# Mamba stage: accumulating transfers for two sums, eight pooled products, and writes on other queues

## The chip, the cores and the metric

The kernel runs on one core of a Trainium2 chip. That core has a matrix engine (TensorE, PE in the profile), three engines for elementwise work (VectorE or DVE, ScalarE or ACT, GpSimd or POOL), and SyncE (SP), which here only issues transfers. Sixteen DMA engines carry the transfers of all queues. Every engine works through its own instructions in order and waits on semaphores for the others. The metric is the device time of one execution in microseconds (us); for the kernel before, the median of three runs is 4138.68, between 4136.19 and 4147.42.

## The reference

The input is one image, 64 x 64 points with 256 channels, in float32. Layer 0 is a group norm, convolutions to q, k and v, attention and a projection. Layer 1 begins with a bidirectional Mamba block over the 4096 points as tokens, and ends with a mixture of experts. The change lies in the Mamba block, of which each direction computes, for 512 inner channels d and 16 states s:

```python
dt = jax.nn.softplus(jnp.einsum('blr,dr->bld', dt, dt_proj_w) + dt_proj_b)
A = -jnp.exp(A_log)
dA = jnp.exp(dt[..., None] * A)
dBx = dt[..., None] * Bm[:, :, None, :] * xc[..., None]
def step(h, inp):
    dA_t, dBx_t, C_t = inp
    h = dA_t * h + dBx_t
    y = jnp.einsum('bds,bs->bd', h, C_t)
    return (h, y)
```

Here xc is the input after a short convolution and silu, and Bm, Cm and the first factor of dt come from one projection of xc. The softplus is computed as relu(v) plus a correction plus log(1 + exp(-|v|)); the sum with that logarithm is one of the sums of the title. After both directions, m = forward + backward goes through a norm and a small two-layer network p, and the token becomes x1 + m + p, with x1 the block's input; the sum with x1 is the other one.

## The kernel before

The kernel has four stages, one after the other: convolutions, attention, Mamba (`mamba_phase`), experts. The change touches `mamba_phase` and the helper `layer_norm` (L101).

The 4096 tokens are cut into 8 chunks of 512. A **turn** i (0 to 15) is one chunk in one direction. A turn has 32 **slots**, one for each group of states and channels: e (4 groups of 128 channels), k (4 groups of states) and j (0 or 2), so that one slot covers two tiles of 128 x 512. The number of a slot in its turn is called `at`. For slot n the functions do the following:

- `inflow(n)` (L1853, its product L1859) is GpSimd's product dbx = (dt times x) times B. It is issued two slots ahead and has three buffers.
- `decay(n)` (L1841, L1849) is ScalarE's exponential da, issued one slot ahead.
- `recur(n)` (L1865) is VectorE's scan (L1872) over 1024 elements, and its product of the states with C (L1877). In the slots of the set `POOLED` the scan writes straight into the tile h, and GpSimd does the product with C one slot later (`pooled`, L1879).
- `sum_states` (L1905) sums the states on TensorE into y, and `close` (L1919) multiplies y by z on VectorE at the end of each e.
- `carry` (L1448) brings the old state into the next turn. It has a product on GpSimd (part 0), an exponential on ScalarE (part 1) and a second product on GpSimd (part 2). It needs the first value of dt of each row, which GpSimd copies to `first` (L1430), and which travels to DRAM-side rows and back to all partitions (L1433, `load_first` L1442).

`prepare(q)` (L1324) is a generator that computes what turn q needs, one step in each slot of the turn before and in the last five of the turn before that. Near its end it takes the logarithm (L1401, slot 23), and then spreads `dt_piece` over slots 24 to 29: with v = 0 GpSimd adds the logarithm to dt (L1425), with v = 1 it multiplies dt by xc (L1436) and adds a large number to the first column of odd rows (L1438), and SP writes both products to the scratch `dtd` in DRAM (L1440). Two of the four pieces with v = 1 are left to slots 2 and 4 of turn q itself. `load_dt` (L1473) reads `dtd` back, each row to four partitions, into the tiles dtr (for `decay`) and dtxr (for `inflow`), three buffers each. For the next group e it is issued at k = 1 and k = 2, slots 3 and 5 of each eight. The writes of B and C to the scratch `bcd` (L1367) and the loads from it (L1469) are on SP's queue also.

`tail(c)` (L1504) is the small network of a chunk, spread over two turns in slots where the set `FULL` allows the engine that its next step names. It has two `layer_norm`s, and each sends a row of 512 values through DRAM-side rows (L127, L129) to have the power taken on 128 partitions (L132). x1 is loaded by SP (L1510) and added to m by GpSimd (L1517).

The order of instructions on all engines is the order in which the program issues them (`manual_schedule`); nothing is moved by a planner. Turn 0 is prepared by `start` (L1551) instead of `prepare`, with parts of its work on VectorE.

Of the kernel before, what the change touches and what calls it, by code (L numbers as in the profile page):

```python
# [14 lines left out]
FP = mybir.dt.float32  # L15
# [4 lines left out]
ALU = mybir.AluOpType  # L20
AX = mybir.AxisListType
# [3 lines left out]
P = 128  # L25
# [3 lines left out]
CT = C // P  # L29
N = 512  # L30
NCH = NT // N
# [6 lines left out]
ET = DI // P  # L38
DS = 16
# [22 lines left out]
def step(gen, n=1):  # L62

    for _ in range(n):
        if gen is None or next(gen, StopIteration) is StopIteration:
            return False
    return True
# [30 lines left out]
        return self.small[:, a : a + n]  # L98


def layer_norm(cx, pool, new_psum, src, dst, mul=None, rest=0, centred=False):  # L101

    nc = cx.nc
    xc = src
    if not centred:  # L110
        ps = new_psum()
        for t in range(CT):
            nc.tensor.matmul(ps, cx.mean_mat, src[:, t, :], start=t == 0, stop=t == CT - 1)
        yield "DVE"
        xc = pool.tile([P, CT, N], FP, name="ln_xc", tag="ln_xc", bufs=1)
        nc.vector.tensor_tensor(xc, src, ps[:, None, :].to_broadcast([P, CT, N]), ALU.subtract)
    yield "ACT"
    nc.scalar.activation(dst, xc, AF.Square)
    yield "PE"
    ps = new_psum()  # L120
    for t in range(CT):
        nc.tensor.matmul(ps, cx.mean_mat, dst[:, t, :], start=t == 0, stop=t == CT - 1)
    yield "ACT"
    rstd = pool.tile([P, N], FP, name="ln_rstd", tag="ln_rstd", bufs=1)
    nc.scalar.activation(rstd[0:1, :], ps[0:1, :], AF.Identity, bias=cx.eps[0:1, :])
    row = cx.rows.tile([1, N], FP, name="ln_row", tag="ln_row", bufs=2)
    nc.sync.dma_start(out=row, in_=rstd[0:1, :])  # L127
    few = pool.tile([P, N // P], FP, name="ln_few", tag="ln_few", bufs=1)
    nc.sync.dma_start(out=few, in_=row.rearrange("o (p j) -> (o p) j", p=P))  # L129
    for at in range(1 + rest):  # L130
# [1092 lines left out]
def mamba_phase(cx, early, w_in, w_x, w_out, w1, w2, x1d, ud, bcd, dtd, x2d, u2d, usum):  # L1223
# [11 lines left out]
    nc, tc = cx.nc, cx.tc  # L1235
    with ExitStack() as ctx:
        one = ctx.enter_context(tc.tile_pool(name="c_one", bufs=1))
# [14 lines left out]
        halos = one.tile([P, 2, ET, 3], FP, name="halos")  # L1252
        nc.gpsimd.memset(halos, 0.0)

        odd = one.tile([P, 2], FP, name="odd")
        nc.vector.tensor_reduce(odd, cx.ident.rearrange("p (a b) -> p b a", b=2), AX.X, ALU.add)
        nc.vector.tensor_scalar(odd[:, 1:2], odd[:, 1:2], 1e33, None, ALU.mult)
        nc.vector.memset(odd[:, 0:1], 0.0)
        for d in range(2):
            for lst, have, src, shape, nm in (  # L1260
                (win, early.win, w_in, [P, CT, 2 * DI], "win"), (wx, early.wx, w_x, [P, ET, DR + 2 * DS], "wx"),
# [5 lines left out]
                t_ = one.tile(shape, FP, name=f"{nm}{d}")  # L1267
# [53 lines left out]
        def few():  # L1321
            return sp.tile([P, N], FP, name="few", tag="few", bufs=3)

        def prepare(q):  # L1324
# [38 lines left out]
            xd = few()[0:nx, :]  # L1363
            nc.scalar.copy(xd, ps[0:nx, :])

            at = 0 if d else DR
            nc.sync.dma_start(out=bcd[q], in_=xd[at : at + 2 * DS, :])  # L1367
            yield


# [31 lines left out]
            zs = in_pair(q, ET)  # L1402
            yield
            got["dt"] = dt
            for at, (v, e) in enumerate(((0, 0), (1, 0), (0, 1), (0, 2), (0, 3), (1, 1))):
                if at == 3 and q > 1:
                    load_first(q, 0)
                dt_piece(q, v, e, ex)
                if at in (0, 2):
                    z = sp.tile([P, 2, N], FP, name="z", tag="z", bufs=3)  # L1410
                    got.setdefault("z", []).append(z)
                if at < 4:
                    nc.scalar.copy(z[:, at % 2, :], zs[at % 2])  # L1413
                if at == 1:
                    zs = in_pair(q, ET + 2)
                    if q + 1 < 2 * NCH:
                        load_u(q + 1)
                yield

        def dt_piece(q, v, e, ex=None, eng=nc.gpsimd):  # L1420


            dt, xc = gots[q]["dt"], gots[q]["xc"]
            if v == 0:
                eng.tensor_tensor(dt[:, e, :], dt[:, e, :], ex[:, e, :], ALU.add)  # L1425
                if q < 2:
                    return
                if e == 0:
                    firsts[q] = ip.tile([P, ET], FP, name="first", tag="first", bufs=1)
                nc.gpsimd.tensor_tensor(firsts[q][:, e : e + 1], dt[:, e, 0:1], odd[:, 0:1], ALU.add)  # L1430
                if e % 2:
                    first_rows[q, e // 2] = cx.rows.tile([P, 2], FP, name="first_row", tag="first_row", bufs=2)
                    nc.sync.dma_start(out=first_rows[q, e // 2], in_=firsts[q][:, e - 1 : e + 1])  # L1433
            else:
                x = few()
                eng.tensor_tensor(x, dt[:, e, :], xc[:, e, :], ALU.mult)  # L1436

                eng.tensor_tensor(dt[:, e, 0:1], dt[:, e, 0:1], odd[:, 1:2], ALU.add)  # L1438
                for w, piece in enumerate((dt[:, e, :], x)):
                    nc.sync.dma_start(out=dtd[2 * q + w][e].rearrange("p j n -> (p j) n"), in_=piece)  # L1440

        def load_first(q, h):  # L1442

# [28 lines left out]

        def load_dt(i, e, j):  # L1473

            tiles = []
            for v, nm in enumerate(("dtr", "dtxr")):
                t_ = dtp.tile([P, 2, N], FP, name=nm, tag=nm)
                rows = dtd[2 * i + v][e, :, j : j + 2, :].rearrange("p j n -> p (j n)")
                nc.sync.dma_start(
                    out=t_.rearrange("p j n -> p (j n)"), in_=rows[:, None].to_broadcast([32, 4, 2 * N])  # L1480
                )
                tiles.append(t_)
            dts[i, e, j] = tiles

        def output(i):
# [18 lines left out]
        def tail(c):  # L1504

            m = m_of[c]
            hn = tl.tile([P, CT, N], FP, name="hn", tag="hn")
            yield from layer_norm(cx, tl, tl_psum, m, hn, nc.gpsimd, 2)
            x1 = tl.tile([P, CT, N], FP, name="x1", tag="ln_xc")
            nc.sync.dma_start(out=x1, in_=x1d[c])  # L1510
            for t in range(CT):
                nc.scalar.activation(
                    hn[:, t, :], hn[:, t, :], AF.Identity, scale=cx.col("lng", t), bias=cx.col("lnb", t)
                )
            yield "DMA"
            yield "POOL"
            nc.gpsimd.tensor_tensor(m, x1, m, ALU.add)  # L1517
            yield "PE"
            a1 = [
                tl.tile([P, 2, N], FP, name="a1a", tag="ln_xc"), tl.tile([P, 2, N], FP, name="a1b", tag="a1b"),  # L1520
# [1 line left out]
            for f in range(FT):  # L1522
# [5 lines left out]
                a = a1[f // 2][:, f % 2, :]  # L1528
# [3 lines left out]
            x2 = m  # L1532
# [10 lines left out]
                )  # L1543
            nc.sync.dma_start(out=x2d[c], in_=x2)
            u2 = tl.tile([P, CT, N], FP, name="u2", tag="hn")
            yield from layer_norm(cx, tl, tl_psum, x2, u2, nc.gpsimd, 2)
            nc.sync.dma_start(out=u2d[c], in_=u2)
            nc.vector.tensor_reduce(usum[:, :, c : c + 1], u2, AX.X, ALU.add)
            yield "DMA"
# [285 lines left out]
            (i, e, k, j) for i in range(2 * NCH) for e in range(ET) for k in range(SQ) for j in (0, 2)  # L1835
        ]
        SPS = ET * SQ * 2
        firsts, first_rows, got_first, brought = {}, {}, {}, {}
        gots, bcs, dts, m_of, das, us, ys, hs = {}, {}, {}, {}, {}, {}, {}, {}

        def decay(n):  # L1841
# [79 lines left out]
            nc.vector.tensor_tensor(g[:, e, :], ys.pop((i, e)), z[e // 2][:, e % 2, :], ALU.mult)  # L1921

        there = set()
        CARRY = {30: (0, 0), 31: (0, 2), 9: (1, 0), 11: (1, 2)}


        POOLED = {4, 10, 12, 18, 28}

        AHEAD = 5

# [11 lines left out]
        with tc.manual_schedule(engines=ORDERED):  # L1942
# [4 lines left out]
            tails, prep, out, last = [], None, None, None  # L1947
            for n, (i, e, k, j) in enumerate(slots):
                at = n % SPS
# [42 lines left out]
                if at >= SPS - AHEAD and i + 2 < 2 * NCH:  # L1992
                    coming = coming or prepare(i + 2)
                    step(coming)
                if i > 0 and at in (2, 4):
                    dt_piece(i, 1, 2 if at == 2 else 3)
                if at == 1 and i > 1:
                    load_first(i, 1)
                elif at in (10, 30) and 1 < i + (at > 16) < 2 * NCH:
                    carry(i + (at > 16), at < 16, 1)  # L2000
                if i == 2 * NCH - 1 and at in (4, 5, 6, 7, 10, 11, 12, 13, 15, 19, 21, 23, 25, 27, 28, 29, 30):
                    last = last or ahead()
# [314 lines left out]
```

## Time and profile before

| what | us |
|---|---|
| median of 3 runs | 4138.68 |
| the profiled execution's own time | 4145.32 |
| its span, first to last instruction | 4143.5 |
| TensorE busy in the span | 3629.8 |
| VectorE busy | 3490.9 |
| ScalarE busy | 2665.3 |
| GpSimd busy | 1748.2 |
| Mamba scans, first to last start | 1964.8 to 3832.1 |

A row of the profile names a source line, an engine, an operation and the tiles written and read. It then gives the shape and the count, and after the bar the busy time in us, the mean of one in ns, and the idle time of the engine just before these instructions with what ended it. Rows of a timeline begin with the start and the duration in us. The time from the issue of a transfer to its landing is known in this trace for those that GpSimd issues.

### The profile page before, as it was taken

The page shows a single profiled execution, that of the slowest core. Times are in us where ns is not written, and L with a number is a line of the kernel's source. Part 1 is how long each engine was busy: PE and PEld are TensorE (multiplying, and loading weights), DVE is VectorE, ACT ScalarE, POOL GpSimd, SP SyncE. Part 2 cuts the span into 40 slices and gives each one's busy share as a digit, 9 for nine tenths or more (in the row PEclk, how much of TensorE's full clock was granted, in tenths as well). Part 3 has the DMA queues.
Part 4 walks back from the last instruction along what each step waited for, and adds up shares of the span by engine and source line. Part 5 has one row for each costly group of instructions (what it writes and reads, how often), then busy time and mean ns, then how long its engine had stood idle before and what let it go on. Part 6 is the DMA issues. An engine that isn't in the chain of part 4 may idle for free. (4 is left out here: it accounts for less than half of the span.)

```text
span 4143.5 us, 43697 instructions
## 1 busy us (share of the span) xinstructions
PE 3629.8 (88%) x15176; PEld 1192.0 (29%) x15176; DVE 3490.9 (84%) x2886; ACT 2665.3 (64%) x4146; POOL 1748.2 (42%) x1189
## 2 busy tenths in 40 slices
PE   6769888999999999998888888888888888876898
PEld 2223332222222222222222222222222232221343
DVE  8998787889879879778899999999999999999211
ACT  1111226878878878776777778778787778775122
POOL 3020000000000000000888889888898989887000
PEclk9889998999999999999889899888989899888899
DMA  6232213000000000002334344343334444432221
GB/s 206 93 111 94 69 65 129 11 27 19 17 24 19 17 24 19 11 22 86 110 114 131 116 123 133 117 126 119 121 109 125 131 120 121 132 110 84 75 67 38
DMA packets 150517, 350.68 MB, mean 85 GB/s; under 512 B 35477, under 2 KB 44437, under 8 KB 150030
## 3 DMA queue, kind: packets, MB, share of 16 engines
q1 hardware_dynamic: 139198, 312.65, 24.6%
q0 software_dynamic: 11088, 35.14, 2.5%
q8 instruction: 121, 1.98, 0.2%
q14 instruction: 110, 0.90, 0.1%
HBM read 268.16 MB, written 79.56 MB: 84 GB/s over the span
## 5 line engine op out<-in xcount | busy, mean ns | idle before, releaser
L1859 POOL TENSOR_TENSOR dbx<-dtxr,b 128x1024 f32<-128x1024 f32 x512 | 1202.7, 2360 | 200.9 <-DMA dtxr<-dtd 106.3
L1016 ACT ACTIVATE e<-sc 128x1024 f32<-128x1024 f32 x1024 | 992.5, 1023 | 200.3 <-PE sc L1009 158.2
L1872 DVE TENSOR_TENSOR_SCAN da<-da,state,dbx 128x1024 f32<-128x1024 f32 x432 | 1014.4, 2348 | 19.4 <-ACT da L1849 7.0
L935 DVE TENSOR_TENSOR s<-s,e 128x1024 f32<-128x1024 f32 x768 | 881.1, 1224 | 45.1 <-ACT e L1016 44.7
L1849 ACT ACTIVATE da<-dtr,aneg 128x512 f32<-128x512 f32 x1024 | 708.2, 692 | 38.4 <-DMA dtr<-dtd 9.1
L1009 PE MATMUL sc<-q,kS 32*128 32x512 f32 x4096 | 652.1, 642 | 11.7 <-ACT e L1016 7.2
L132 POOL TENSOR_TENSOR ln_few<-ln_few,minus_half 128x4 f32<-128x4 f32 x29 | 29.5, 1017 | 1407.7 <-DMA ln_few<-ln_row 1407.7
L1877 DVE TENSOR_TENSOR h<-da,c 128x1024 f32<-128x1024 f32 x432 | 529.2, 1225 | 33.1 <-PE y L1912 1.2
L942 PE MATMUL av<-e,vT 128*32 128x512 f32 x4096 | 548.1, 606 | 3.7 <-ACT o L948 3.7
L1912 PE MATMUL y<-h,sel 128*32 128x512 f32 x2048 | 373.9, 665 | 97.4 <-DVE h L1877 71.6
L453 PE MATMUL cv<-v,u 128*128 128x512 f32 x928 | 412.4, 605 | 27.9 <-DVE pad L274 13.8
L1009 PEld LDWEIGHTS sc<-q,kS 32*128 32x128 f32 x4096 | 211.2, 183 | 455.3 <-issue 233.5
L1306 PE MATMUL mm<-u,win 128*128 128x512 f32 x464 | 253.7, 697 | 77.2 <-ACT z L1413 33.1
L453 PEld LDWEIGHTS cv<-v,u 128*128 128x128 f32 x928 | 178.8, 194 | 259.2 <-issue 226.8
L551 DVE SCALAR_TENSOR_TENSOR acc<-pad,wdw_s,acc 128x768 f32<-128x768 f32 (+1 forms) x192 | 236.0, 1234 | 19.9 <-ACT acc L544 14.2
L1903 ACT COPY state<-da 128x2 f32<-128x2 f32 x431 | 67.9, 158 | 257.4 <-DVE h L1877 256.2
L1352 PE MATMUL mm<-xp,taps 128*128 128x512 f32 x480 | 212.8, 595 | 0.0
L935 DVE TENSOR_TENSOR s<-e 128x1024 f32<-128x1024 f32 x128 | 151.2, 1225 | 65.3 <-ACT e L1016 65.1
L1872 DVE TENSOR_TENSOR_SCAN h<-da,state,dbx 128x1024 f32<-128x1024 f32 x80 | 187.5, 2344 | 11.0 <-ACT state L1903 9.8
L942 PEld LDWEIGHTS av<-e,vT 128*32 128x32 f32 x4096 | 81.2, 108 | 395.4 <-issue 377.7
L1882 POOL TENSOR_TENSOR h<-h,c 128x1024 f32<-128x1024 f32 x80 | 188.3, 2354 | 1.0 <-ACT state L1903 1.0
L1912 PEld LDWEIGHTS y<-h,sel 128*32 128x32 f32 x2048 | 56.6, 113 | 380.5 <-DVE h L1877 163.7
(381 smaller groups left out, 3933.4 us busy)
## 6 DMA issues: line engine op xcount, KB each, us to landing
dtr<-dtd SPq DMA_DIRECT2D x128, 512.0 KB
dtxr<-dtd SPq DMA_DIRECT2D x128, 512.0 KB
b<-bcd SPq DMA_DIRECT2D x64, 256.0 KB
c<-bcd SPq DMA_DIRECT2D x64, 256.0 KB
dtd<-dt SPq DMA_DIRECT2D x64, 256.0 KB
dtd<-few SPq DMA_DIRECT2D x64, 256.0 KB
u<-uv SPq DMA_DIRECT2D x24, 640.0 KB
uv<-wo POOLq DMA_DIRECT2D x60, 128.0 KB, 3.1
```

What stands on the lines that cost most here:

```text
L453: nc.tensor.matmul(rows4(ps), u[:, dy, P * ci : P * ci + P], v[:, dy : dy + HR, ci, :], start=dy + ci == 0, stop=dy == k - 1 and ci == CT - 1,
L551: nc.vector.scalar_tensor_tensor(o, src, w_ap, o, ALU.mult, ALU.add)
L935: nc.vector.tensor_tensor(z, x, y, ALU.add)
L942: nc.tensor.matmul(g.av[32 * h : 32 * h + 32, :], vT[:, kb, P * t + 32 * h : P * t + 32 * h + 32], es[h // 2][:, h % 2, :], start=kb == 0, ...
L1009: nc.tensor.matmul(ps[h // 2][:, h % 2, :], kS[r, t, P * kb : P * kb + P], q_t[r, t, :], start=True, stop=True,)
L1016: nc.scalar.activation(e, ps[i], AF.Exp)
L1306: nc.tensor.matmul(ps, win[d][:, t, P * e : P * e + P], u[:, t, ::-1] if d else u[:, t, :], start=t == 0, stop=t == CT - 1,)
L1849: nc.scalar.activation(da[:, v, :], dts[i, e, j][0][:, v, :], AF.Exp, scale=aneg[i % 2][:, a : a + 1])
L1859: nc.gpsimd.tensor_tensor(u, dts[i, e, j][1], bcs[i, k][0][:, None, :].to_broadcast([P, 2, N]), ALU.mult)
L1872: nc.vector.tensor_tensor_scan(das[n].rearrange("p v n -> p (v n)"), da.rearrange("p v n -> p (v n)"), u.rearrange("p v n -> p (v n)"), st ...
L1877: nc.vector.tensor_tensor(h, da, bcs[i, k][1][:, None, :].to_broadcast([P, 2, N]), ALU.mult)
L1912: nc.tensor.matmul(ys[i, e][32 * j : 32 * j + 32, :], cx.sel, hs[n + j // 2][:, j % 2, :], start=False, stop=k == SQ - 1,)
```

## The change

The sum of dt and the logarithm is no longer four operations on GpSimd but two transfers that GpSimd issues, each of half of the channels, that add in passing. So is the sum of m and x1. `POOLED` grows from 5 slots of 32 to 8. The first values are copied by `keep_firsts`, two columns at once. Products and writes of `dt_piece` become two functions, `dt_times_x` and `write_dt`, and the writes are issued later, with the product ahead of dt. `load_dt` loads dtxr ahead of dtr. The write of B and C, and in the tail the first row of a norm, are issued by ScalarE. Two steps of the carry move from slot 30 to 29, and one from 10 to 9.

```diff
@@ layer_norm
-    nc.sync.dma_start(out=row, in_=rstd[0:1, :])
+    (queue or nc.sync).dma_start(out=row, in_=rstd[0:1, :])
@@ prepare
-            nc.sync.dma_start(out=bcd[q], in_=xd[at : at + 2 * DS, :])
+            nc.scalar.dma_start(out=bcd[q], in_=xd[at : at + 2 * DS, :])
...
-            for at, (v, e) in enumerate(((0, 0), (1, 0), (0, 1), (0, 2), (0, 3), (1, 1))):
+            for at in range(6):
+                if at == 0:
+                    for es in (slice(0, 2), slice(2, ET)):
+                        nc.gpsimd.dma_start(out=dt[:, es, :], in_=ex[:, es, :], accum_op=ALU.add)
                 if at == 3 and q > 1:
                     load_first(q, 0)
-                dt_piece(q, v, e, ex)
+                if at in (2, 4):
+                    keep_firsts(q, at // 4)
+                if at in (2, 5):
+                    dt_times_x(q, at // 3)
+                if at == 2:
+                    write_dt()
...
+        def keep_firsts(q, h):
+            if q < 2:
+                return
+            firsts = ip.tile([P, 2], FP, name="first", tag="first")
+            nc.gpsimd.tensor_copy(firsts, gots[q]["dt"][:, 2 * h : 2 * h + 2, 0])
+            first_rows[q, h] = cx.rows.tile([P, 2], FP, name="first_row", tag="first_row", bufs=2)
+            nc.sync.dma_start(out=first_rows[q, h], in_=firsts)
+
+        def dt_times_x(q, e, eng=nc.gpsimd):
+            dt, xc = gots[q]["dt"], gots[q]["xc"]
+            x = few()
+            eng.tensor_tensor(x, dt[:, e, :], xc[:, e, :], ALU.mult)
+            eng.tensor_tensor(dt[:, e, 0:1], dt[:, e, 0:1], odd, ALU.add)
+            unwritten.append((q, e, x))
+
+        def write_dt():
+            for q, e, x in unwritten:
+                for w, piece in ((1, x), (0, gots[q]["dt"][:, e, :])):
+                    nc.sync.dma_start(out=dtd[2 * q + w][e].rearrange("p j n -> (p j) n"), in_=piece)
+            unwritten.clear()
@@ load_dt
-            for v, nm in enumerate(("dtr", "dtxr")):
+            for v, nm in ((1, "dtxr"), (0, "dtr")):
@@ tail
-            yield from layer_norm(cx, tl, tl_psum, m, hn, nc.gpsimd, 2)
-            x1 = tl.tile([P, CT, N], FP, name="x1", tag="ln_xc")
-            nc.sync.dma_start(out=x1, in_=x1d[c])
+            yield from layer_norm(cx, tl, tl_psum, m, hn, nc.gpsimd, 2, queue=nc.scalar)
...
-            yield "DMA"
             yield "POOL"
-            nc.gpsimd.tensor_tensor(m, x1, m, ALU.add)
+            nc.gpsimd.dma_start(out=m, in_=x1d[c], accum_op=ALU.add)
@@ the loop over slots
-        CARRY = {30: (0, 0), 31: (0, 2), 9: (1, 0), 11: (1, 2)}
-        POOLED = {4, 10, 12, 18, 28}
+        CARRY = {29: (0, 0), 31: (0, 2), 9: (1, 0), 11: (1, 2)}
+        POOLED = {2, 4, 10, 12, 16, 18, 26, 28}
...
+                if at in (3, 5, 30):
+                    write_dt()
                 if i > 0 and at in (2, 4):
-                    dt_piece(i, 1, 2 if at == 2 else 3)
+                    dt_times_x(i, 2 if at == 2 else 3)
...
-                elif at in (10, 30) and 1 < i + (at > 16) < 2 * NCH:
+                elif at in (9, 29) and 1 < i + (at > 16) < 2 * NCH:
                     carry(i + (at > 16), at < 16, 1)
```

`dt_piece` itself is kept for turn 0, where it calls the two new functions.

More of the change, by code (lines that the diff above doesn't have):

```diff
@@ L98, in col, with layer_norm @@
         return self.small[:, a : a + n]
-def layer_norm(cx, pool, new_psum, src, dst, mul=None, rest=0, centred=False):
+def layer_norm(cx, pool, new_psum, src, dst, mul=None, rest=0, centred=False, queue=None):
     nc = cx.nc
@@ L1253, in mamba_phase @@
         nc.gpsimd.memset(halos, 0.0)
[L1255 to L1258, printed above, removed]
+        odd = one.tile([P, 1], FP, name="odd")
+        nc.vector.tensor_reduce(odd, cx.ident.rearrange("p (a b) -> p b a", b=2)[:, 1:2, :], AX.X, ALU.add)
+        nc.vector.tensor_scalar(odd, odd, 1e33, None, ALU.mult)
         for d in range(2):
@@ L1418, in prepare @@
                 yield
+        def keep_firsts(q, h):
[16 more added lines that the diff above has]
+            unwritten.clear()
         def dt_piece(q, v, e, ex=None, eng=nc.gpsimd):
-            dt, xc = gots[q]["dt"], gots[q]["xc"]
             if v == 0:
+                dt = gots[q]["dt"]
                 eng.tensor_tensor(dt[:, e, :], dt[:, e, :], ex[:, e, :], ALU.add)
[L1426 to L1433, printed above, removed]
-            else:
[L1435 to L1440, printed above, removed]
+            else:
+                dt_times_x(q, e, eng)
+                write_dt()
         def load_first(q, h):
@@ L1473, in load_dt @@
         def load_dt(i, e, j):
-            tiles = []
-            for v, nm in enumerate(("dtr", "dtxr")):
-                t_ = dtp.tile([P, 2, N], FP, name=nm, tag=nm)
+            tiles = {}
+            for v, nm in ((1, "dtxr"), (0, "dtr")):
+                t_ = tiles[v] = dtp.tile([P, 2, N], FP, name=nm, tag=nm)
                 rows = dtd[2 * i + v][e, :, j : j + 2, :].rearrange("p j n -> p (j n)")
@@ L1481, in load_dt @@
                 )
-                tiles.append(t_)
             dts[i, e, j] = tiles
@@ L1545, in tail @@
             u2 = tl.tile([P, CT, N], FP, name="u2", tag="hn")
-            yield from layer_norm(cx, tl, tl_psum, x2, u2, nc.gpsimd, 2)
+            yield from layer_norm(cx, tl, tl_psum, x2, u2, nc.gpsimd, 2, queue=nc.scalar)
             nc.sync.dma_start(out=u2d[c], in_=u2)
@@ L1837, in mamba_phase @@
         SPS = ET * SQ * 2
-        firsts, first_rows, got_first, brought = {}, {}, {}, {}
+        first_rows, got_first, brought, unwritten = {}, {}, {}, []
         gots, bcs, dts, m_of, das, us, ys, hs = {}, {}, {}, {}, {}, {}, {}, {}
@@ L1994, in mamba_phase @@
                     step(coming)
+                if at in (3, 5, 30):
+                    write_dt()
                 if i > 0 and at in (2, 4):
-                    dt_piece(i, 1, 2 if at == 2 else 3)
+                    dt_times_x(i, 2 if at == 2 else 3)
                 if at == 1 and i > 1:
                     load_first(i, 1)
-                elif at in (10, 30) and 1 < i + (at > 16) < 2 * NCH:
+                elif at in (9, 29) and 1 < i + (at > 16) < 2 * NCH:
                     carry(i + (at > 16), at < 16, 1)
```

## The prediction

> **What bounds the kernel now.** The change lies in the Mamba stage, so I read the page's engine rows and groups, then a table of stretches for that stage, then the waits of VectorE and GpSimd in it, then the timeline at one seam. The page:
>
> ```profile
> PE 3629.8 (88%) x15176; PEld 1192.0 (29%) x15176; DVE 3490.9 (84%) x2886; ACT 2665.3 (64%) x4146; POOL 1748.2 (42%) x1189
> ...
> L1859 POOL TENSOR_TENSOR dbx<-dtxr,b 128x1024 f32<-128x1024 f32 x512 | 1202.7, 2360 | 200.9 <-DMA dtxr<-dtd 106.3
> ...
> L1882 POOL TENSOR_TENSOR h<-h,c 128x1024 f32<-128x1024 f32 x80 | 188.3, 2354 | 1.0 <-ACT state L1903 1.0
> ```
>
> The shares are averages over four stages and mislead: GpSimd's 42% is nearly all in one stage. One product with C costs 2.354 us on GpSimd and 1.225 on VectorE. A turn i of 32 slots is bounded by the activation of z that opens it (L1988); its starts cut the stage. Columns: length, then busy us of each engine, granted clock, DMA share, GB/s:
>
> ```profile
> core 0: us, PE busy (x) PEld busy (x) DVE busy (x) ACT busy (x) POOL busy (x), PEclk, DMA share, GB/s
> ...
> 2660.72:2779.57 118.85, 103.06 (x286) 34.29 (x283) 114.03 (x71) 90.36 (x175) 103.01 (x64) 0.87 0.42 122
> ...
> 3013.14:3128.30 115.16, 98.53 (x280) 31.96 (x278) 111.03 (x68) 92.99 (x181) 103.84 (x65) 0.88 0.40 122
> ```
>
> Turns are read from 2086.47 to 3718.28, 14 of them: 1631.8/14 = 116.6 us each. VectorE is busy 112.1 of that, GpSimd about 102, ScalarE about 91. VectorE sets the pace, and GpSimd has only 14 us in hand. The groups of those 14 turns:
>
> ```profile
> L1872 DVE TENSOR_TENSOR_SCAN h<-da,state,dbx 128x1024 f32<-128x1024 f32 x70 | 164.1, 2344 | 10.6 <-ACT state L1903 9.8 <-ACT dbx L1897 0.7
> L1877 DVE TENSOR_TENSOR h<-da,c 128x1024 f32<-128x1024 f32 x378 | 463.0, 1225 | 29.2 <-PE y L1912 1.2 <-DVE da L1872 0.5
> ...
> L1425 POOL TENSOR_TENSOR dt<-dt,ex 128x512 f32<-128x512 f32 x56 | 66.2, 1182 | 0.0
> L1430 POOL TENSOR_TENSOR first<-dt,odd 128x1 f32<-128x1 f32 x56 | 10.6, 189 | 4.4
> ```
>
> and GpSimd's waits in them (total, times, longest):
>
> ```profile
> POOL dbx L1859 <- DMA dtxr<-dtd: 79.6, 30, 6.5
> POOL dbx L1859 <- DVE da L1872: 52.4, 41, 3.3
> POOL brought L1461 <- ACT state L1903: 30.6, 5, 6.5
> ```
>
> VectorE itself waits 34.5 us for others (2.5 a turn); the rest of its idle time, 2 us a turn, is the small gap before each product.
>
> **Part 1, three more products a turn on GpSimd (5 to 8).** A scan followed by its product takes 3.51 to 3.58 us to the next scan; a scan whose product is pooled takes 2.25 (scans at 2764.87, 2767.13, 2770.64 and 2071.70, 2073.95, 2077.53). Saved: about 1.28 each, 3 x 1.28 = 3.84 us a turn while VectorE is the bound. Against it: a pooled scan writes straight into h and waited 9.8 us over 70 for ScalarE, 0.14 each, so +0.4 a turn. GpSimd gets 3 x 2.33 (2.354 less overlap) = +7.0.
>
> A rule speaks against this part. The Trainium skill, "SBUF — State Buffer", "SBUF: two separate sides", says that a VectorE operation with two SBUF inputs and a GpSimd operation that reads SBUF exclude one another for a whole instruction. Scan and product both have such inputs. By the rule 48 products would cost 48 x (2.35 - 1.28) = +51 us. The row denies it: 114.03 busy on VectorE and 103.01 on GpSimd fit into the same 118.85 us, so they overlap. I take the row.
>
> **Part 2, dt + log as two accumulating transfers.** Removed from GpSimd a turn: 4 x 1.18 and 4 x (0.19 + 0.08 gap) = 5.8. Added: two copies of first values, 0.4, and two issues. GpSimd issues in the trace, the first from the line that loads x1 in the stage's start, the second from the writes of u in the conv stage (then their landings):
>
> ```profile
> L1556 POOL DMA_DIRECT2D x<-x1d x1: 597/597/597, 1941.0 to 1941.0; - x1
> DMA to landing us min/median/max: 4.2/4.2/4.2
> ...
> L295 POOL DMA_DIRECT2D uv<-wo x60: 540/540/560, 72.0 to 302.4; - x60
> DMA to landing us min/median/max: 2.0/2.7/7.7
> ```
>
> The issue stays at 0.54 although VectorE is at work then, so I take 0.6 each, 1.2 a turn. No accumulating transfer is in the trace. From 128 KB in 2.7 and 512 KB in 4.2: 2.2 fixed and 2.0 per 512 KB. As a plain copy it lands in 4.2 (lower bound). The Trainium skill, "Collectives: The Full Stack", "The bandwidth ceiling: the fold count and why AG ≠ RS ≠ AR", has a transfer that adds read two sources, at about half a copy's rate: 2.2 + 4.0 = 6.2 for the first (estimate), 10.2 for the second behind it. Upper bound 12.2, the longest landing of any GpSimd load here (L284). I take 6.2, stretched to about 8 because the 16 engines are already 0.4 busy.
>
> Is that covered? GpSimd works in order, so the copy of first values (slot 26) holds up all inflows behind it, which the scans need. The timeline at that seam, before:
>
> ```profile
> 2747.30 1.92 ACT L1401 ACTIVATE ex<-ex 128x2048 f32<-128x2048 f32 x1
> ...
> 2750.19 1.26 POOL L1425 TENSOR_TENSOR dt<-dt,ex 128x512 f32<-128x512 f32 x1
> ...
> 2755.60 2.36 POOL L1859 TENSOR_TENSOR dbx<-dtxr,b 128x1024 f32<-128x1024 f32 x1
> ...
> 2764.87 2.34 DVE L1872 TENSOR_TENSOR_SCAN h<-da,state,dbx 128x1024 f32<-128x1024 f32 x1
> ```
>
> Issue at 2750.2; the inflow of slot 26 starts at 2755.5, as its buffer comes free with scan 25, and ends at 2757.9. So a landing up to 7.7 us is covered by inflows. Wait w: 0 at the lower bound, 4.5 at the upper, 0.6 taken.
>
> **Part 3, the chain of first values and the carry.** Carry 0 moves from slot 30 to 29, while the write of e0 moves from 25 to 26. SP in order: write of e0 issued 2759.5, landed 2.3 later (in the start 1949.35 issue, 1951.65 the load that waits for it), dtxr and dtr 1.2, then the first values at about 2763.6. They land at 2766 alone, or at 2768 behind the two loads (dtxr issued 1952.59 was used at 1958.97). GpSimd, recounted from the inflow of 2747.9 with the new order, reaches the carry at 2766.8. Wait v: 0 to 4 (below nothing is excluded, nobody waits there now), 0.7 taken. Then inflow, pooled product, product of e1, inflow: it ends at 2775.5 + w + v, while scan 0, moved up by 1.28, wants it at 2776.5. That turn has a 1.2 us operation of the tail in between, the turns beside it do not, so the slack averages 0.4: VectorE loses 0.6 + 0.7 - 0.4 = 0.9 a turn. In slots 2 to 5 GpSimd then does four inflows (9.3), two products with x (2.9) and two pooled products (4.7), 16.9 us, while VectorE needs 2.26 + 3.56 + 2.26 + 3.56 = 11.6; before it was 14.6 against 13. Three buffers let GpSimd run about 5 us ahead of need, so this uses up the lead by slot 8: 0.4 a turn (0 to 1.5).
>
> **Part 4, queues, x1.** The write of B and C (SP 0.32) and one row of each norm (0.24, two a pair of turns) go to ScalarE: +0.6, with waits on its own results perhaps +1 a turn. ScalarE has about 25 us free a turn, 14.5 of it in its wait for VectorE's product, so nothing; without that cover 1 to 1.6 a turn. SP loses its block at that write and gets dtxr ahead of dtr, so dtxr leaves about 0.6 us earlier and no longer behind a wait for ScalarE; GpSimd's 79.6 us of waits shrink. VectorE waited only 6.8 us for GpSimd in all 14 turns, so this is worth 0.3 a turn. ScalarE's exponentials one slot earlier shorten the 30.6 us at L1461, also GpSimd's. x1: GpSimd loses 2.35 and gains 0.6 per two turns; m is wanted several slots later, so the landing is hidden (without cover about 6 us per two turns).
>
> **Sum.** GpSimd: 102 + 7.0 - 5.8 + 0.4 + 1.2 - 0.9 = 104. VectorE a turn: -3.84 + 0.4 + 0.9 + 0.4 - 0.3 = -2.4, to 114.2, so GpSimd keeps 10 us for its own waits, which were 8.6. Fourteen turns: -34. Turn 0 is held by the start and keeps its sums: 0. The last has no preparation: -3.4, less some wait at its end. In all about -36: 4145.3 of the profiled execution (span 4143.5) becomes 4109. It lies 6.6 above the median shown, so 4138.7 becomes 4103.
>
> **Rivals.** (a) GpSimd keeps up everywhere: no w, no v, no loss at slot 8. 15.5 x 3.84 = 60, so 4079. For it: 10 us of slack; against: the lead at the seam is spent. (b) The effects cancel: w + v near 3.9 instead of 1.3, 14 x 2.6 = 36 lost again, so 4139. (c) Slower: the accumulation lands late. Each us of wait is 14 us in all, and from w + v = 3.9 on the kernel is slower than before. At the upper bound 12.2, w = 4.5 and v = 0.7: 3.9 more than assumed, 14 x 3.9 = 55, so 4158; with v = 2 as well, 4176. For it: the accumulation's rate is not in the trace and the copy heads GpSimd's queue; against: 7.7 us of cover. (d) The transfers change nothing and VectorE's waits merely move to ScalarE: it has 25 us, unlikely.
>
> **How the numbers follow.** Chances: forecast 0.42 (its own range 4088 to 4126), (a) 0.17, (b) 0.14, (c) 0.27. Under 0.3% (12.4 us) a measurement of this kernel tells nothing. Faster 0.59, within 0.14, slower 0.27. The range runs from (a)'s 4078 to 4178, which leaves out the worst of (c).
>
> **What would show it.** Right: turns near 114 us, 128 products on L1882, GpSimd about 104 of them busy, the copy of first values waiting about 0.6 for the accumulation, the first carry product 0.7 for its row. Wrong: landings over 8 us, a wait of several us at the copy or at the first dbx of a turn, GpSimd operations longer than 2.36, or VectorE waiting over 5 us a turn for dbx.

## The result, and the profile after

The changed kernel takes 4214.5 us (median of 4 runs, 4213.7 to 4215.8) where the kernel before, measured with it, takes 4139.5: a ratio of 1.0181, with a 95% interval of 1.0168 to 1.0194. It is 75 us slower, where the prediction had 36 us faster and a range that ended at 4178.

The page of the changed kernel has VectorE 58 us less busy and GpSimd 64 us more, so the work moved as it was meant to (GpSimd's product with C is now L1897, 128 of them; dbx is L1874, the scans L1887):

```profile
PE 3605.0 (86%) x15176; PEld 1191.8 (28%) x15176; DVE 3432.6 (81%) x2837; ACT 2663.3 (63%) x4146; POOL 1811.9 (43%) x1179
...
L1897 POOL TENSOR_TENSOR h<-h,c 128x1024 f32<-128x1024 f32 x128 | 303.5, 2371 | 8.2 <-ACT state L1918 7.9
```

The loss lies in the turns, above all at the passage from one turn to the next, called a seam below. The activations of z that open them (L2003) now run from 2090.05 to 3785.84, so that a turn takes 121.1 us, 4.5 more than before; TensorE's granted clock over these turns is 0.88, as before. Two turns in the table of stretches:

```profile
2814.64:2939.34 124.70, 103.85 (x291) 35.04 (x291) 108.42 (x66) 92.55 (x181) 107.10 (x64) 0.88 0.42 124
3059.90:3181.13 121.23, 97.04 (x289) 32.81 (x288) 108.36 (x66) 92.92 (x182) 107.06 (x64) 0.94 0.44 127
```

VectorE's busy time fell by 3.4 us a turn (1568.9/14 before, 1520.9/14 after), about what was forecast, and still the turn grew. Neither VectorE nor GpSimd fills it any more: both wait. Over the 14 turns, VectorE's waits first (total, times, longest):

```profile
DVE da L1887 <- ACT dbx L1912: 57.7, 39, 5.1
DVE da L1887 <- ACT state L1918: 46.4, 13, 7.1
DVE h L1887 <- ACT state L1918: 14.7, 18, 1.3
```

then GpSimd's, then ScalarE's:

```profile
POOL brought L1475 <- DMA first_r<-first_row: 115.6, 14, 10.3
...
ACT brought L1477 <- POOL brought L1475: 83.5, 14, 8.3
ACT dbx L1912 <- POOL brought L1480: 64.1, 14, 5.3
```

VectorE's 34.5 us of waits have become some 150, from 2.5 to 10.6 us a turn. GpSimd's wait for dtxr (79.6 us) is gone. In its place stands one wait in every turn, 115.6/14 = 8.3 us, for the row of first values at the first product of the carry. ScalarE's exponential of the carry waits for that product, and everything behind it on ScalarE waits too. That is how the row comes through to VectorE. The timeline at one seam (start, duration):

```profile
2910.71 0.33 SPq L1314 DMA_DIRECT2D u<-ud  x1
2911.14 0.52 SPq L1488 DMA_DIRECT2D b<-bcd  x1
2911.75 0.55 SPq L1488 DMA_DIRECT2D c<-bcd  x1
2912.40 0.54 SPq L1434 DMA_DIRECT2D first_row<-first  x1
2913.03 0.38 SPq L1449 DMA_DIRECT2D dtd<-few  x1
2918.11 0.18 POOL L1432 COPY first<-dt 128x2 f32<-128x2 f32 x1
2920.99 0.53 SPq L1498 DMA_DIRECT2D dtxr<-dtd  x1
2921.62 0.54 SPq L1498 DMA_DIRECT2D dtr<-dtd  x1
2922.26 1.91 SPq L1465 DMA_DIRECT2D first_r<-first_row  x1
2927.46 0.22 POOL L1475 TENSOR_TENSOR brought<-aneg,first_r 128x16 f32<-128x16 f32 x1 [9.17 <-DMA first_r<-first_row]
2927.72 0.21 ACT L1477 ACTIVATE brought<-brought 128x16 f32<-128x16 f32 x1 [6.29 <-POOL brought L1475]
2930.36 2.36 DVE L1887 TENSOR_TENSOR_SCAN da<-da,state,dbx 128x1024 f32<-128x1024 f32 x1 [3.62 <-ACT state L1918]
2936.32 0.29 ACT L1912 ACTIVATE dbx<-dbx,brought 128x1 f32<-128x1 f32 x1 [4.50 <-POOL brought L1480]
2936.65 2.36 DVE L1887 TENSOR_TENSOR_SCAN da<-da,state,dbx 128x1024 f32<-128x1024 f32 x1 [2.61 <-ACT dbx L1912]
```

GpSimd is ready for the carry at 2918.3 and starts it at 2927.5. SP issued the write of e0 (`dtd<-few`) at 2913.0 and stood still until it had landed, 8 us later, since the load of dtxr reads it. Only behind that load and dtr's did it issue the load of the first values, whose own store had gone out at 2912.4. Ahead of the write stand the loads of u, b and c, 1 MB issued within 2 us. At the same place in the kernel before, the write went ahead of them:

```profile
2755.93 0.43 SPq L1440 DMA_DIRECT2D dtd<-few  x1
2758.74 0.32 SPq L1315 DMA_DIRECT2D u<-ud  x1
2759.11 0.53 SPq L1469 DMA_DIRECT2D b<-bcd  x1
2759.73 0.55 SPq L1469 DMA_DIRECT2D c<-bcd  x1
2760.38 0.54 SPq L1433 DMA_DIRECT2D first_row<-first  x1
2761.02 0.52 SPq L1479 DMA_DIRECT2D dtr<-dtd  x1
```

When such a write landed can be read from the updates of its semaphore in the trace: 2.31 to 2.54 us after its issue at the 14 seams of the kernel before, 4.7 to 8.0 (mean 7.1) in the changed one.

In the changed kernel the wait then runs through the exponential (6.29) to scan 31 (3.62), and through part 2 of the carry and ScalarE's `bring` (4.50) to scan 0 (2.61).

What was doubted most came out well. The transfers that add, all 30, with their landings:

```profile
L1407 POOL DMA_DIRECT2D dt<-ex x30: 1205/1272/1719, 2063.4 to 3754.1; - x30
...
DMA to landing us min/median/max: 5.1/5.9/7.2
```

Landing 5.9 against an estimate of 6.2 to 8, and no wait at the copy of first values.

### The profile page after: what moved, and what is told of

It is laid out like the page before. It is cut to its first block, busy times and chain, and to the rows that moved or that the text cites. A ratio compares the mean times of both kernels' runs of the same rounds, so it can differ in the third digit from the quotient of the medians.

```text
span 4212.1 us, 43868 instructions
## 1 busy us (share of the span) xinstructions
PE 3605.0 (86%) x15176; PEld 1191.8 (28%) x15176; DVE 3432.6 (81%) x2837; ACT 2663.3 (63%) x4146; POOL 1811.9 (43%) x1179
## 3 DMA queue, kind: packets, MB, share of 16 engines
q1 hardware_dynamic: 137442, 307.97, 22.9%
## 5 line engine op out<-in xcount | busy, mean ns | idle before, releaser
L1874 POOL TENSOR_TENSOR dbx<-dtxr,b 128x1024 f32<-128x1024 f32 x512 | 1219.9, 2403 | 119.2 <-DVE da L1887 53.8
L1887 DVE TENSOR_TENSOR_SCAN da<-da,state,dbx 128x1024 f32<-128x1024 f32 x384 | 901.2, 2347 | 125.6 <-ACT dbx L1912 58.0
L1892 DVE TENSOR_TENSOR h<-da,c 128x1024 f32<-128x1024 f32 x384 | 470.3, 1225 | 29.9 <-PE y L1927 0.6
L1927 PE MATMUL y<-h,sel 128*32 128x512 f32 x2048 | 344.4, 674 | 105.0 <-POOL h L1897 83.2
L1887 DVE TENSOR_TENSOR_SCAN h<-da,state,dbx 128x1024 f32<-128x1024 f32 x128 | 300.1, 2344 | 36.7 <-ACT state L1918 15.6
L1897 POOL TENSOR_TENSOR h<-h,c 128x1024 f32<-128x1024 f32 x128 | 303.5, 2371 | 8.2 <-ACT state L1918 7.9
L1912 ACT ACTIVATE dbx<-dbx,brought 128x1 f32<-128x1 f32 x392 | 110.4, 282 | 91.7 <-POOL brought L1480 64.1
L1305 PEld LDWEIGHTS mm<-u,win 128*128 128x128 f32 x464 | 96.2, 218 | 221.7 <-issue 101.8
```

The costliest lines, as they stand in the source:

```text
L1305: nc.tensor.matmul(ps, win[d][:, t, P * e : P * e + P], u[:, t, ::-1] if d else u[:, t, :], start=t == 0, stop=t == CT - 1,)
L1874: nc.gpsimd.tensor_tensor(u, dts[i, e, j][1], bcs[i, k][0][:, None, :].to_broadcast([P, 2, N]), ALU.mult)
L1887: nc.vector.tensor_tensor_scan(das[n].rearrange("p v n -> p (v n)"), da.rearrange("p v n -> p (v n)"), u.rearrange("p v n -> p (v n)"), st ...
L1892: nc.vector.tensor_tensor(h, da, bcs[i, k][1][:, None, :].to_broadcast([P, 2, N]), ALU.mult)
L1897: nc.gpsimd.tensor_tensor(hs[n], hs[n], bcs[i, k][1][:, None, :].to_broadcast([P, 2, N]), ALU.mult)
L1927: nc.tensor.matmul(ys[i, e][32 * j : 32 * j + 32, :], cx.sel, hs[n + j // 2][:, j % 2, :], start=False, stop=k == SQ - 1,)
```

## The experiments

Theory R (row): the first values are late because their load stands behind the write of e0, which the change put into a later slot, and the carry was moved ahead at the same time. Rivals: theory A (the adding transfers hold GpSimd or the DMA queues), theory P (three more products are too much for GpSimd), the moves to ScalarE's queue, and, after the first four runs, theory S (VectorE waits for ScalarE at slots 0 to 2 on account of pooled slots and late loads).

The results together. "Turn" is the mean distance of equal scans over turns 2 to 15, from the starts of the scans; "31 to 3" is the part of it in the five steps from scan 30 to scan 3; "write" is the mean time from the issue of e0's write (the product with x) to its landing; "row" is the mean of the waits of GpSimd that the profile puts down to first_r (12 to 14 of them, one a turn). The ratio is to the kernel before on the same chip.

| kernel | ratio, 95% interval | turn | 31 to 3 | write | row |
|---|---|---|---|---|---|
| before | 1 | 117.2 | 20.0 | 2.3 | none |
| changed | 1.0181 [1.0168, 1.0194] | 121.5 | 26.0 | 7.1 | 8.3 |
| row's load first | 1.0063 [1.0046, 1.0080] | 118.6 | 22.9 | 7.5 | 3.3 |
| carry in slot 30 | 1.0049 [1.0030, 1.0068] | 118.3 | 22.5 | 7.7 | 2.4 |
| sums on GpSimd | 1.0181 [1.0163, 1.0198] | 121.7 | 26.1 | 7.4 | 7.2 |
| five pooled slots | 1.0221 [1.0204, 1.0238] | 123.7 | 27.3 | 7.7 | 10.9 |
| row first, carry in 30 | 1.0032 [1.0015, 1.0050] | 118.0 | 22.2 | 7.2 | none |
| the same, dtr first | 1.0052 [1.0035, 1.0069] | 119.2 | 22.0 | 7.1 | none |
| u behind the write | 1.0066 [1.0049, 1.0083] | 118.5 | 22.8 | 5.2 | 4.7 |
| queues back | 1.0162 [1.0145, 1.0179] | 121.0 | 25.2 | 7.2 | 7.9 |
| row, carry and u | 1.0006 [0.9997, 1.0016] | 116.6 | 20.8 | 5.2 | none |
| e0 summed early, carry in 30 | 0.9966 [0.9957, 0.9976] | 115.5 | 19.7 | 2.1 | none |
| the same, slot 2 not pooled | 0.9982 [0.9972, 0.9992] | 116.3 | 20.3 | 2.0 | none |
| before with eight pooled slots | 1.0040 [1.0024, 1.0057] | 118.0 | 20.9 | 2.4 | none |

**The row's load ahead of the loads of dt.**

```diff
-                if at == 3 and q > 1:
-                    load_first(q, 0)
...
                     if (k, j) == (1, 2):
+                        if e == ET - 1 and i > 0:
+                            load_first(i + 1, 0)
                         load_dt(*nxt, 0)
```

> The changed kernel, but in slot 27 SP issues the load of the first values (h = 0) ahead of dtxr and dtr, so it no longer waits for the write of e0 to land. Theory R (the carry's row is late behind that write; GpSimd waits 8.3 us a turn for it): the row's own store was issued 9 us ahead of the load, so the load can go at about half of that, the wait falls to 1 to 3 us a turn, turns from 121.1 to about 115.5: 4135 to 4145. Theory A (the accumulating transfers hold GpSimd) and theory P (three more products are too much for GpSimd): no more than 1 us a turn, 4200 to 4215.

Measured 1.0063: about two thirds of the loss is gone, with one transfer issued three places earlier on its queue. GpSimd's wait fell from 8.3 to 3.3 us each time. Theories A and P allowed for 1 us a turn at most. Theory R's own figure was not reached, though (4135 to 4145 is 1.0013 at most). Ahead of the two loads the row landed 2.2 us after its issue instead of 5.2, but it was issued only 1.9 us earlier than in the changed kernel: it now waited for its own 1 KB store, which also stands behind u, b and c and landed 7.2 us after its issue.

**The carry back in slot 30.**

```diff
-        CARRY = {29: (0, 0), 31: (0, 2), 9: (1, 0), 11: (1, 2)}
+        CARRY = {30: (0, 0), 31: (0, 2), 9: (1, 0), 11: (1, 2)}
...
-                elif at in (9, 29) and 1 < i + (at > 16) < 2 * NCH:
+                elif at in (9, 30) and 1 < i + (at > 16) < 2 * NCH:
```

(The exponential for h = 1 stayed in slot 9 in this run, where the expectation has it in 10.)

> The changed kernel, with carry part 0 for h = 0 back in slot 30 (and its exponential with it, and the one of h = 1 back in 10). Theory R: GpSimd has an inflow, a pooled product and the product of e1 to do first, 6.1 us more, so the wait falls from 8.3 to about 2 us a turn; the exponential then comes later for part 2 in slot 31, which gives some back: 4135 to 4160. Theories A and P: within 10 us of 4214.

Measured 1.0049, with waits of 2.4 us for the row; that is the upper end of theory R's figure. So the same loss can be cut from the other end, by asking for the row one slot later. What is left of GpSimd's waits for the row, and a wait of ScalarE that came up:

```profile
POOL brought L1475 <- DMA first_r<-first_row: 30.8, 13, 4.5
...
ACT da L1864 <- DMA dtr<-dtd: 28.4, 15, 4.2
```

**The sums on GpSimd instead of transfers**, at the same place.

```diff
-                        nc.gpsimd.dma_start(out=dt[:, es, :], in_=ex[:, es, :], accum_op=ALU.add)
+                        nc.gpsimd.tensor_tensor(dt[:, es, :], dt[:, es, :], ex[:, es, :], ALU.add)
```

> The changed kernel, with the two accumulating transfers of dt replaced at the same place by two sums on GpSimd (128 x 1024, 2.36 us each instead of two issues of 1.44 us). Theory A: the transfers and their traffic are what costs, so 4140 to 4170. Theory R: the first values are ready no earlier in SP's order and GpSimd has 1.8 us a turn more to do in front of its wait, which covers it: 4205 to 4225. Theory P: 25 us slower, 4240.

The ratio is that of the changed kernel to the fourth digit. Theory A falls: the transfers did not cause the loss, and without them the write lands as late (7.4 us). They brought no gain in this place either, where GpSimd has the wait for the row to spare.

**Five pooled slots, as before.**

```diff
-        POOLED = {2, 4, 10, 12, 16, 18, 26, 28}
+        POOLED = {4, 10, 12, 18, 28}
```

> The changed kernel, with the set of pooled slots as before (5 of 32). Theory P: GpSimd is relieved of 7 us a turn and the loss goes, 4135 to 4150. Theory R: VectorE gets 3.84 us a turn back, but part of it lies in the wait at the seam; the row stays late by 6 to 10 us: 4205 to 4250. Theory A: 4210 to 4250 as well.

Slower still, 1.0221. Theory P falls as the cause: in the changed kernel the three slots save about 17 us (0.0040 of the time).

**Both cures of the row.** The edits of the first two runs together.

> Both cures of the row at once: its load ahead of dtxr and dtr in slot 27, and carry part 0 of h = 0 back in slot 30. Theory R: the wait for first_r (8.3 us a turn as changed, 2.2 to 2.8 with one cure) goes to 0, and another 10 to 20 us of the whole come back from 4170: 4145 to 4160, ratio 1.000 to 1.004. A second theory S: the rest lies at slots 0 to 2, where VectorE waits for ScalarE (29 to 35 us at scan 2 in the runs with one cure), and the row has no more part in it: 4160 to 4170.

Measured 1.0032; the row's wait is gone, and yet the turn is 118.0 us. What is left is at scan 2: VectorE waits 33 us there over the turns for ScalarE, and ScalarE waits 53.9 us for dtr, against 6.4 before the change.

**dtr ahead of dtxr again**, in addition.

```diff
-            for v, nm in ((1, "dtxr"), (0, "dtr")):
+            for v, nm in ((0, "dtr"), (1, "dtxr")):
```

> The same, and dtr is loaded ahead of dtxr again. Theory S, with dtr's lateness as its cause (ScalarE waited 28 to 36 us for dtr with one cure, 6.4 before the change): that wait falls below 10 us, scan 2 waits under 1 us a turn, and the run gains 10 to 25 us over the run without this edit. If the order of the two loads does not matter: within 5 us of it.

Not faster: 1.0052, against 1.0032 with overlapping intervals. Neither a gain of 10 to 25 us nor a difference within 5 came, but 10 us more, not clear of noise. The wait at scan 2 went, as theory S had it, from 33 to 2 us, but 31 us came up at scan 1, where GpSimd's dbx is late. ScalarE's wait for dtr fell from 53.9 to 21.5 us, and GpSimd's for dtxr rose from 46.8 to this:

```profile
POOL dbx L1872 <- DMA dtxr<-dtd: 114.3, 40, 7.0
```

The order of the two loads only chooses who waits. Both come late as a pair, and that points back to the writes which they read.

**u behind the write of e0**, in the changed kernel and alone.

```diff
                 if at == 2:
                     write_dt()
+                    if q + 1 < 2 * NCH:
+                        load_u(q + 1)
...
                     zs = in_pair(q, ET + 2)
-                    if q + 1 < 2 * NCH:
-                        load_u(q + 1)
```

> The changed kernel, but the load of u (512 KB) is issued behind the writes of e0 instead of ahead of them. If the writes land late because they stand in the rings behind u, b and c (1 MB): from the issue of x's write to the load of dtxr 8 us become 4 to 6 and the wait for first_r falls by 2 to 3 us a turn; u comes late for slot 27, which may cost on TensorE: 4175 to 4220. If the delay has another cause, the 8 us stay.

This recovers nearly two thirds of the loss: 1.0066. The time from the write to the load that waits for it fell from 7.1 to 5.2 us, and the row's wait with it:

```profile
POOL brought L1475 <- DMA first_r<-first_row: 65.3, 14, 6.9
```

The edit also let b be issued earlier, about 11 us or more ahead of the write, since b no longer stood behind u, so that c alone is just ahead of it (2.5 us at most seams). The changed kernel has a seam of its own that fits: the one into the last turn loads no u, and there the write landed in 4.7 us, where the other 13 took 6.6 to 8.0. So the write's landing depends on what SP issued ahead of it, and the loss follows the landing. Whether it waits for its place in the queue or for free DMA engines, no run tells apart: at the seam shown the 16 engines were 0.91 busy from 2912.5 to 2917.0. The price that was feared, TensorE waiting for u, was there (39.1 us), and cost less than the cure brought.

**The moves to ScalarE's queue undone.**

```diff
-            nc.scalar.dma_start(out=bcd[q], in_=xd[at : at + 2 * DS, :])
+            nc.sync.dma_start(out=bcd[q], in_=xd[at : at + 2 * DS, :])
...
-            yield from layer_norm(cx, tl, tl_psum, m, hn, nc.gpsimd, 2, queue=nc.scalar)
+            yield from layer_norm(cx, tl, tl_psum, m, hn, nc.gpsimd, 2)
```

(and the same in the second norm of the tail)

> The changed kernel, with the write of B and C and the first row of the tail's norms back on SP's queue. If the moves to ScalarE cost: faster by 10 us or more. By theory R they have little part: 4205 to 4225.

1.0162, with an interval that overlaps that of the changed kernel: some 8 us of the 75, not clear of noise.

**Row, carry and u together.**

> All three cures in the changed kernel: the row's load ahead of dtxr and dtr, carry part 0 of h = 0 in slot 30, and the load of u behind the writes of e0. The write then lands 2 us earlier (from its issue to the load of dtxr 5.2 us where it was 7.1), so dtr comes earlier and ScalarE's wait for it (54 us over the turns with two cures) falls below 25. Theory R with S: 4125 to 4145, ratio 0.997 to 1.001. If TensorE's wait for a late u (39 us with the third cure alone) comes through to VectorE: above 1.003, no better than with two cures.

1.0006 [0.9997, 1.0016], no different from before. The cures together take the loss away. What keeps it there is probably u, which TensorE waits for (31.1 us): VectorE's products wait 28.4 us for TensorE's sums, and the step to scan 31 takes 5.6 us instead of 4.0.

**e0 summed and written as early as before, the rest of the change kept, carry in slot 30.**

```diff
                 if at == 0:
-                    for es in (slice(0, 2), slice(2, ET)):
+                    nc.gpsimd.tensor_tensor(dt[:, 0, :], dt[:, 0, :], ex[:, 0, :], ALU.add)
+                    for es in (slice(1, 2), slice(2, ET)):
                         nc.gpsimd.dma_start(out=dt[:, es, :], in_=ex[:, es, :], accum_op=ALU.add)
+                    if q > 1:
+                        early_first[q] = ip.tile([P, 2], FP, name="first", tag="first")
+                        nc.gpsimd.tensor_copy(early_first[q][:, 0:1], dt[:, 0, 0:1])
+                if at == 1:
+                    dt_times_x(q, 0)
+                    write_dt()
...
-                if at in (2, 5):
-                    dt_times_x(q, at // 3)
-                if at == 2:
-                    write_dt()
+                if at == 5:
+                    dt_times_x(q, 1)
```

(`keep_firsts` then copies only e1 into that tile for h = 0.)

> The changed kernel, but e0 of dt is summed on GpSimd in slot 24 and its product and write stay in slot 25, ahead of u, as before the change; only e1 to e3 are summed by the transfers, and carry part 0 of h = 0 is in slot 30. If the loss came from moving e0's write past u, b and c and the carry with it, and eight pooled slots are worth their 3.84 us a turn less the waits for ScalarE: 4100 to 4125, ratio 0.991 to 0.997, with no wait for first_r and dtxr loaded at once. If the transfers themselves cost VectorE something: above 1.000.

0.9966 [0.9957, 0.9976]: 4125.4 us, faster than both kernels. SP's queue at one of its seams shows the order that the change had given up. The write stands ahead of u, b and c, and the loads of dt follow as soon as they are issued:

```profile
2749.23 0.33 SPq L1458 DMA_DIRECT2D dtd<-few  x1
2749.66 0.38 SPq L1458 DMA_DIRECT2D dtd<-dt  x1
2751.77 0.32 SPq L1314 DMA_DIRECT2D u<-ud  x1
2752.14 0.53 SPq L1497 DMA_DIRECT2D b<-bcd  x1
2752.76 0.55 SPq L1497 DMA_DIRECT2D c<-bcd  x1
2753.40 0.54 SPq L1443 DMA_DIRECT2D first_row<-first  x1
2754.03 0.52 SPq L1507 DMA_DIRECT2D dtxr<-dtd  x1
2754.66 0.54 SPq L1507 DMA_DIRECT2D dtr<-dtd  x1
2759.57 0.51 SPq L1474 DMA_DIRECT2D first_r<-first_row  x1
```

GpSimd waits for no row, and its wait for dtxr is down to 9.7 us. It only just met its expectation (0.991 to 0.997 was expected, and 0.9966 is at the end of it).

**The same without slot 2.**

> The same without slot 2 in the pooled set (7 of 32). In slot 2 VectorE waited 33 us over the turns with two cures, because ScalarE has two table loads and z in slots 0 and 1 and a pooled scan gives it 1.3 us less. If that slot gives nothing: within 5 us of the run with slot 2. If it still gains: 8 to 18 us slower.

0.9982, 5.3 us slower by the medians, which lies between the two cases that were expected: the slot is worth some 0.4 us a turn, not 1.28. (The profiled executions give 0.8 a turn, but that of this run was 6 us above its median.) Three pooled slots do not pay three times the mean.

**The kernel before with eight pooled slots and nothing else.**

> The kernel before with nothing but the eight pooled slots. GpSimd has 102 + 7 = 109 us of work a turn and waits of its own of about 8, together as long as the turn. If VectorE stays the bound: 4085 to 4110. If GpSimd's room is what the transfers had to make: 4125 to 4160, with VectorE waiting for dbx at slots 0 to 3.

1.0040, slower. Here VectorE waits 23 us for ScalarE at scan 0, and ScalarE waits for GpSimd (51.9 us for dbx and 48.4 us for the carry, where it was 18.2 and 14.5). Pooled slots alone lose 17 us against before; with the sums of e1 to e3 off GpSimd, and the rest of the change, they gain 14. It is likely that they need the room which the transfers make on GpSimd, but no run takes the transfers alone out of the fast kernel.

## Why the prediction was wrong

**What bounds the kernel, and part 1** held in their mechanism. VectorE lost 3.4 us a turn of busy time, and scans and products of GpSimd still overlap: 108.42 and 107.10 us busy in 124.70, with a product at 2371 ns where it was 2354. But the rule that I weighed there (the Trainium skill, "SBUF — State Buffer", "SBUF: two separate sides") was misapplied: it speaks of VectorE operations with two inputs in SBUF, and da lies in a PSUM pool, so scan and product have one tile in SBUF each (the scan a column of state besides). The overlap was rightly read from the row; it says nothing against the rule, and no run here tests it. Mis-sized was the term of +0.4 a turn for pooled scans that wait for ScalarE. Scans into h waited 31.8 us in the 14 turns of the changed kernel, 2.3 a turn (1.7 of it for ScalarE), where they waited 0.76 before. I multiplied the mean wait of five slots by three. The new slot 2, though, is where ScalarE has z and two table loads to do, and a pooled scan gives it 1.3 us less time: the run without slot 2 puts that slot's gain at 0.4 us a turn where 1.28 were counted.

**Part 2** was right where it was least certain. The landing was 5.9 us (the estimate from half a copy's rate was 6.2; no plain copy between the same tiles was measured), w was 0, and the rival that I took for the road to a slower kernel (a late accumulation) did not happen. The two issues were undercharged: together they take about 2.5 us instead of 1.2, and the dbx behind the second takes 3.3 us instead of 2.36, so 3.4 us a turn. It cost nothing, as the run with the sums on GpSimd shows.

**Part 3 is the step that failed**, at v, "0 to 4, 0.7 taken". It measured 8.3 us a turn. The waits were looked for in the right chain: write of e0, dtxr, dtr, first values, carry. One term in it was wrong: "landed 2.3 later", taken from the stage's start. At its old place the write did land in 2.3 us; at its new one it lands 6.6 to 8.0 us after its issue, and 4.7 in the last turn. Moving it from slot 25 to 26 put it behind the loads of u, b and c on SP's queue, 1 MB in all, and the prediction never named these. It listed the queues that writes were moved to, but for the one write that moved in time it did not ask what it was now behind. With 7.1 instead of 2.3, v comes to 0.7 + 4.8 = 5.5, beyond the upper bound of 4, and the forecast turns from 36 us faster to about 31 us slower by the same arithmetic, without any new mechanism.

The rest of the 8.3 is two smaller terms, both means over the 14 seams. The row lands 5.2 us after the issue of its load, behind the two loads of dt, where 2.4 to 4.4 were allowed. GpSimd is ready for the carry 5.4 us after the write's issue, not 7.3. A link was missing too: the row's load waits for the row's own store, which landed 6.5 us after its issue in the kernel before (6.8 in the changed one), so the row would have come some 2 us later than forecast even behind a quick write (an estimate: 6.5 after a store issued 0.6 ahead of the write is 5.9, where the prediction has the load 4.1 after the write). In the run with the row's load first, that store is what the row still waits for.

The slack of 0.4 in front of scan 0 was too simple as well. The delay reached VectorE by two roads, the second through ScalarE's exponential: 3.6 us more at scan 31 and 2.6 us more at scan 0 (steps of 7.5 and 6.3 us instead of 3.9 and 3.7).

**Part 4**: moves to ScalarE cost some 8 us in all, not clear of noise. dtxr ahead of dtr did end GpSimd's 79.6 us of waiting, but that was no gain, since ScalarE then waited for dtr once the row was cured. **The sum**: turn 0 was booked at 0. From its first scan to the next turn's it takes 7.6 us longer (127.5, 119.9 before), but that scan starts 4.0 us earlier, so 3.6 us are lost. Which part of the change costs them stays open.

The account, from the starts of the scans: the first 4.0 us earlier, turn 0 7.6 longer, turn 1 6.3, turns 2 to 14 13 x 4.5 = 58; that is 68, and the spans of the two profiled executions differ by 68.6. The medians differ by 75, since the profiled execution of the kernel before was 6 us above its median.

What stays open: the run that beats both kernels gains about 14 us, where rival (a) of the prediction had 60. The waits for ScalarE at scans 2, 3, 12 and 29 and for TensorE at scan 16, about 43 us over 14 turns, are the largest visible part of the rest; no run took them away.

## What to carry to other kernels

When a write is moved later, price its landing at its new place in the queue, with the bytes that are now issued ahead of it, and not with the landing at the old one. Then follow who stands behind its reader on the issuing queue: here a 1 KB row waited for a 256 KB write that it had nothing to do with, and its own store stood behind the same 1 MB of loads. A small transfer that a chain of engines waits for goes ahead of large ones that have time, and a step should not be moved earlier in the same change that makes its input later.

## What the runs showed of the hardware that was not expected

A write of 256 KB to DRAM landed 2.3 us after its issue where SP had issued nothing but another write in the ten us ahead of it (14 seams of the kernel before). It took 4.7 where c (256 KB) had been issued 2.5 us ahead (the last turn of the changed kernel), 5.2 where u went out right behind it in addition (the run with u behind), and 7.3 on average behind u, b and c, 1 MB in 2.3 us (the other 13 seams). A store of 1 KB that stood behind the same three loads took 6.5 us in the kernel before. SP's waits in the changed kernel's 14 turns have the write as a line that before did not exist (22 loads of dt that stood waiting for such a write, at the seams and elsewhere; the total is the time that SP stood still):

```profile
SPq L1498 <- DMA dtd<-few: 99.7, 22, 7.1
```

A transfer of 512 KB that adds float32 from SBUF into SBUF landed in 5.9 us (5.1 to 7.2). From x1 in DRAM it was 5.4, where the plain load took 4.2. Two such issues together hold GpSimd for about 2.5 us, where a plain one took 0.54 to 0.60, and the dbx right behind the second took 3.29 to 3.35 us instead of 2.36 in 14 of 15 turns (2.88 in the other). With sums in place of the transfers, no dbx took over 2.69.
